# A four-layer convolution, attention and scan kernel: layer 2's products with C moved to GpSimd, its sums over states to adding transfers, softmax reciprocals sent through DRAM

## The chip, the cores and the metric

The kernel runs on one core of a Trainium2 chip. The metric is the device time of one execution in microseconds (us). A core has five engines that matter here: PE (TensorE, matmuls; its weight loads are counted apart as PEld), DVE (VectorE), ACT (ScalarE), POOL (GpSimd) and SP, which here only issues transfers. Each engine works through its own instructions strictly in the order of the program. Sixteen DMA engines move data. "Granted clock" is the mean TensorE clock that the throttle granted, as a share of full speed.

## The reference, cut to what matters

The input has 4 images of 128 channels and 64 x 64 pixels. Four layers follow one another:

```python
x = attention(x)         # layer 0: q, k of 16 channels, softmax over 4096 pixels, v of 128; gamma * out + x
x = two_convs(x)         # layer 1: two 3x3 convolutions with 4-bit weights and activations
x = mamba(x)             # layer 2: selective scan, 256 inner channels, 16 states, then group norm, silu, + x
x = attention(x)         # layer 3: the same with 64 channels, then a product with wo, + x
# softmax: p = exp(e); out = (p @ v) / p.sum()          one sum and one reciprocal per pixel
# layer 2, for every inner channel d and state n, over 4096 steps t:
#   h[t] = dA[t] * h[t-1] + dt[t] * x[t] * B[t, n]
#   y[t] += h[t] * C[t, n]                               summed over the 16 states
```

## The kernel before

The program cuts each image in 8 blocks of 512 pixels. Attention (layers 0 and 3) is 512 tiles of work for PE and ACT. Layer 2 is 32 blocks x 16 states = 512 steps `m`, each on a tile of 128 x 1024 (256 channels x 512 pixels). It runs beside the attention and the convolutions of other images. The last image's layer 3 can only run when its layer 2 is done.

The order of instructions on each engine is made ahead, in Python, by a small list scheduler. Every chain of work yields an engine, a time and what it needs; the chain with the earliest start wins, with 0.15 us of handicap for each unit of its rank. A transfer is an operation of 0.1 us on SP with an assumed landing time `lag`. Only the order goes into the program. At run time the hardware keeps the order, whether the assumed times were right or not.

```python
    @staticmethod
    def op(engine, time, *needs, bank=False, table=None, port=False, lag=0.0): ...
    # in run():
                key = start + load + self.RANK * item[0]         # RANK = 0.15
                if best is None or key < best[0]:
                    best = key, start, load, item
    # ... one (rank, chain) pair for each part of the program
            (3, scans()),
            (3, additions()),
            (3, fetches()),
```

Layer 2's step is three chains: DVE multiplies by B, multiplies the step before by C and makes two scans; GpSimd adds the product to y; ACT copies the last column, where the next block's scan starts.

```python
    def lasts():
        # ... for every step m that is not in an image's last block
                yield op("ACT", 0.2, ("s", m, 1))                # after the second scan
                nc.scalar.copy(hlast[:, n, :], hss[m][:, :, TB - 1])
    def readout(m):
        hs = hss[m]
        nc.vector.tensor_mul(hs, hs, bcs.pop(m)[:, 1:2, :].to_broadcast([P, 2, TB]))     # C
    def scans():
        # ... for every step m
            hss[m] = hs = pair("hs", "hs", 3)
            nc.vector.tensor_mul(hs, ud, bcs[m][:, 0:1, :].to_broadcast([P, 2, TB]))     # B
            if m:
                yield op("DVE", 1.22, ("last", m - 1), port=True)
                readout(m - 1)
            for h in range(2):
                nc.vector.tensor_tensor_scan(hs[:, h, :], das.pop((m, h)), hs[:, h, :], ...)
    def additions():
        # ... for every step m
            nc.gpsimd.tensor_tensor(y, y, hss.pop(m), ALU.add)
```

The sums of the softmax lie in rows 0, 32, 64 and 96 of `ss`. PE gathers them into columns, DVE takes the reciprocal, PE spreads it over all rows:

```python
    def finish(s, c, us, ss):
        # 4 matmuls  sc[:, k] = ss[:, 128k : 128k+128].T @ sel4
        nc.vector.reciprocal(r, sc[:, 0:4])
        # 4 matmuls  sc[:, 128k : 128k+128] = broadcast(r[:, k]).T @ ident
        nc.vector.tensor_mul(us, us, sc)
```

Before each accumulation of p @ v, PE also writes zeros to the accumulator with matmuls of a zero tile.

## Time and profile before

| | before |
|---|---|
| median of 3 runs (lowest, highest) | 3715.16 us (3711.8, 3719.31) |
| profiled run, granted clock | 3718.9 us, 0.967 |
| busy in 240 to 3360 us (3120 us): PE, DVE | 2879.0, 2895.0 us |
| DMA share there | 0.40 |

The prediction shows the busy table, three stretches, the chain and the groups that the change removes. Here are three groups that it leaves, as the page's fifth part lists them: line, engine, operation, output from inputs, shapes, count, busy us, mean ns of one, then the idle time just before and its main releaser.

```profile
L1026 DVE TENSOR_TENSOR_SCAN hs<-da,hlast,hs 128x512 f32<-128x512 f32 x896 | 1102.3, 1264 | 45.5 <-ACT da L991 45.2
L1018 DVE TENSOR_TENSOR hs<-ud,bc 128x1024 f32<-128x1024 f32 x512 | 656.9, 1283 | 0.0
L1001 ACT COPY hlast<-hs 128x2 f32<-128x2 f32 x448 | 85.4, 191 | 130.9 <-DVE hs L1026 129.1
```

The product with B takes 1.28 us and the scan 1.26. DVE spends nearly no time waiting in these groups.

### The profile page before, as it was taken

Reading aid. Unit: us, or ns where it says so; the run is one execution under the profiler, and the core shown is the slowest. Engines: PE = TensorE matmul, PEld = TensorE weight load, DVE = VectorE, ACT = ScalarE, POOL = GpSimd, SP = SyncE. Lnnn points to the kernel's source line nnn. Section 1 sums busy time; section 2 is a strip of 40 time slices with the busy share of each in tenths; the row PEclk is TensorE's granted clock in tenths of the full one; section 3 lists DMA queues with packets and bytes.
Section 4 is the critical chain, followed back from the end, with each engine's and each line's share of the span. In section 5 each row is a group of like instructions: output and inputs, shape, how many; then the busy total and the mean of one; then the engine's idle time right before and its main releaser. Section 6 shows DMA issues by size and latency. Waiting matters only on the chain.

```text
span 3718.9 us, 70774 instructions
## 1 busy us (share of the span) xinstructions
PE 3406.0 (92%) x29874; PEld 2235.8 (60%) x29879; DVE 3104.3 (83%) x2944; ACT 2513.0 (68%) x3656; POOL 1314.1 (35%) x568
## 2 busy tenths in 40 slices
PE   5999979989989999999888999999899989998998
PEld 3776656666666666655545666665555545565665
DVE  3369999999999999899988999999789888893333
ACT  3467767777787777777677767767777777774443
POOL 0014434444434444344433444443344444441000
PEclk8999999999999999999999999999999999999999
DMA  2023334333443334443443333343434444331000
GB/s 70 1 53 96 91 103 100 90 95 92 117 102 97 94 87 95 112 107 101 106 114 102 89 91 92 88 112 87 107 95 108 119 91 108 101 104 63 13 19 17
DMA packets 203658, 327.82 MB, mean 88 GB/s; under 512 B 50609, under 2 KB 53441, under 8 KB 203329
## 3 DMA queue, kind: packets, MB, share of 16 engines
q1 hardware_dynamic: 196384, 322.09, 34.7%
q8 instruction: 236, 3.87, 0.4%
q10 hardware_dynamic: 6944, 1.10, 0.2%
q14 instruction: 94, 0.76, 0.1%
HBM read 304.27 MB, written 18.87 MB: 87 GB/s over the span
## 4 chain that ended last, share of the span: by engine, by line
PE 61%; DVE 21%; ACT 10%; issue 5%; DMA 2%; ACTq 0%; SPq 0%; DVEq 0%
PE us L571 25%; PE e L494 14%; DVE hs L1026 9%; PE us L591 7%; DVE hs L1018 4%; DVE hs L1008 3%; PE conv L686 2%; ACT da L991 2%; ACT p L513 2%; PE xh L775 2%; PE sc L651 2%; PE yo L905 1%; PE sc L638 1%; PE proj L465 1%; PE proj L423 1%
## 5 line engine op out<-in xcount | busy, mean ns | idle before, releaser
L1043 POOL TENSOR_TENSOR y<-y,hs 128x1024 f32<-128x1024 f32 x512 | 1215.3, 2374 | 2050.1 <-DVE hs L1008 2033.6
L571 PE MATMUL us<-p,v 128*32 128x256 f32 (+1 forms) x12288 | 1521.7, 389 | 128.3 <-ACT p L513 128.1
L571 PEld LDWEIGHTS us<-p,v 128*32 128x32 f32 (+1 forms) x12288 | 1009.0, 138 | 550.1 <-ACT p L513 153.5
L513 ACT ACTIVATE p<-e 128x1024 f32<-128x1024 f32 x1024 | 1002.0, 1019 | 383.2 <-PE e L494 255.5
L1026 DVE TENSOR_TENSOR_SCAN hs<-da,hlast,hs 128x512 f32<-128x512 f32 x896 | 1102.3, 1264 | 45.5 <-ACT da L991 45.2
L991 ACT ACTIVATE da<-dt,amat 128x512 f32<-128x512 f32 x1024 | 701.1, 690 | 266.8 <-DVE hs L1026 263.0
L1008 DVE TENSOR_TENSOR hs<-hs,bc 128x1024 f32<-128x1024 f32 x512 | 666.9, 1303 | 34.7 <-ACT hlast L1001 33.8
L1018 DVE TENSOR_TENSOR hs<-ud,bc 128x1024 f32<-128x1024 f32 x512 | 656.9, 1283 | 0.0
L494 PE MATMUL e<-it,v 64*128 64x256 f32 x4096 | 534.6, 402 | 9.2 <-ACT p L513 8.2
L494 PEld LDWEIGHTS e<-it,v 64*128 64x128 f32 x4096 | 386.9, 193 | 155.6 <-issue 89.6
L591 PE MATMUL us<-p,ones 128*32 128x256 f32 x7040 | 469.9, 385 | 0.0
L591 PEld LDWEIGHTS us<-p,ones 128*32 128x32 f32 x7040 | 202.4, 110 | 183.6 <-issue 64.5
L535 DVE TENSOR_TENSOR acc<-p 128x1024 f32<-128x1024 f32 x24 | 29.4, 1225 | 225.4 <-PE us L591 192.6
L494 PEld LDWEIGHTS e<-it,j 64*128 64x128 f32 x2048 | 141.5, 190 | 101.9 <-issue 69.1
L494 PE MATMUL e<-it,j 64*128 64x256 f32 x2048 | 196.5, 310 | 5.1 <-ACT p L513 3.4
L1001 ACT COPY hlast<-hs 128x2 f32<-128x2 f32 x448 | 85.4, 191 | 130.9 <-DVE hs L1026 129.1
L535 DVE TENSOR_TENSOR acc<-p,acc 128x1024 f32<-128x1024 f32 x96 | 117.4, 1223 | 61.6 <-ACT p L513 58.1
L1026 DVE TENSOR_TENSOR_SCAN hs<-da,hs 128x512 f32<-128x512 f32 x128 | 149.9, 1204 | 8.6 <-ACT da L991 8.5
L775 PEld LDWEIGHTS <-w 128*128 128x128 bf16 x576 | 51.4, 98 | 98.3 <-issue 54.3
L775 PE MATMUL xh<-x,w 128*128 128x512 fp8e4 x384 | 95.3, 385 | 1.1 <-ACT sz L798 0.4
L1047 POOL TENSOR_TENSOR y<-y,sz 128x1024 f32<-128x1024 f32 x32 | 95.2, 2976 | 2.5
L465 PE MATMUL proj<-L_conv_wvT,x_in 128*128 128x128 f32 (+1 forms) x512 | 67.7, 288 | 22.9 <-DVE it L410 13.2
(162 smaller groups left out, 2617.3 us busy)
## 6 DMA issues: line engine op xcount, KB each, us to landing
bc<-bc_d SPq DMA_DIRECT2D x512, 512.0 KB, 4.9
x_in<-in_x SPq DMA_DIRECT2D x16, 512.0 KB, 4.8
xpad<-in_x SPq DMA_DIRECT2D x32, 256.0 KB, 3.4
x_d<-yo SPq DMA_DIRECT2D x32, 256.0 KB, 2.3
x_in<-x_d SPq DMA_DIRECT2D x16, 512.0 KB, 6.0
o<-x_d SPq DMA_DIRECT2D x32, 256.0 KB, 5.4
out<-o SPq DMA_DIRECT2D x32, 256.0 KB, 2.2
bc_d<-xd SPq DMA_DIRECT2D x64, 32.0 KB, 1.7
```

The lines of the kernel that those rows point to most:

```text
L465: nc.tensor.matmul(to[:, k * d : (k + 1) * d], lhsT=x[:, k // 4, k % 4 * P : (k % 4 + 1) * P], rhs=wv, start=True, stop=True,)
L494: nc.tensor.matmul(e[k % 4 // 2][:, k % 2, k // 4, :], lhsT=jts[s][row : row + D3, col : col + P], rhs=its[s][row : row + D3, c * CB : (c ...
L513: nc.scalar.activation(p, es[t][h], AF.Exp)
L535: nc.vector.tensor_add(accs[k], ps[t, h], other)
L571: nc.tensor.matmul(us[rows, 0, :], lhsT=vts[s][:, 8 * q + k, cols], rhs=ps[t, h][:, k % 2, k // 4, :], start=False, stop=False,)
L591: nc.tensor.matmul(us[32 * m : 32 * m + 32, 1, :], lhsT=ones[:, 0:32], rhs=term, start=False, stop=q == NQ - 1 and k >= len(terms) - 4,)
L775: nc.tensor.matmul(g, lhsT=w3[:, k // len(rhs), lhs[k % len(rhs)] : lhs[k % len(rhs)] + P], rhs=x[:, rhs[k % len(rhs)]], start=(k == 0), s ...
L991: nc.scalar.activation(da, live["in", g][0][:, h, :], AF.Exp, scale=amat[:, h, n : n + 1])
L1008: nc.vector.tensor_mul(hs, hs, bcs.pop(m)[:, 1:2, :].to_broadcast([P, 2, TB]))
L1018: nc.vector.tensor_mul(hs, ud, bcs[m][:, 0:1, :].to_broadcast([P, 2, TB]))
L1026: nc.vector.tensor_tensor_scan(hs[:, h, :], das.pop((m, h)), hs[:, h, :], hlast[:, n, h : h + 1] if g % NTB else 0.0, ALU.mult, ALU.add,)
L1043: nc.gpsimd.tensor_tensor(y, y, hss.pop(m), ALU.add)
```

## The change

Its intent is to take work off DVE (the product with C) and off PE (reciprocals and zero products), to let GpSimd do the product and the DMA engines the sum over states. Ranks and some buffers change with it.

```diff
+    def readouts():
+        for m in range(NM):
+            g, n = divmod(m, DS)
+            yield op("POOL", 2.36, ("s", m, 1), ("last", m), port=True)
+            hs = hss[m]
+            nc.gpsimd.tensor_tensor(
+                hs, hs, bcs.pop(m)[:, 1:2, :].to_broadcast([P, 2, TB]), ALU.mult
+            )
 ...
+            yield op("POOL", 0.9, *need, lag=7.5)
 ...
+            nc.gpsimd.dma_start(
+                out=sums[g][n % 3],
+                in_=hss.pop(m),
+                accum_op=ALU.bypass if n in (1, 2) else ALU.add,
+            )
 ...
+    def gates():                      # DVE adds the three tiles, GpSimd multiplies by silu(z)
 ...
```

The product writes over `hs`, so it has to wait (`("last", m)`) until ACT has copied the last column.

```diff
@@ finish (softmax reciprocals)
-        # the 8 matmuls shown above
+        yield op("SP", 0.1, ("evict", 2 * k + 1), lag=2.2)
+        nc.sync.dma_start(out=s_d, in_=us[0:P:32, 1, :])                       # 4 rows to DRAM
+        yield op("SP", 0.1, ("s_d", k), lag=2.5)
+        nc.sync.dma_start(out=st, in_=s_d.rearrange("g (p e) -> p g e", e=4))  # back, 128 rows
+        yield op("DVE", 0.3, ("st", k))
+        nc.vector.tensor_reduce(r, st.rearrange("p g e -> p e g"), AX.X, ALU.add)
+        nc.vector.reciprocal(r, r)
+        yield op("SP", 0.1, lag=2.2)
+        nc.sync.dma_start(out=r_d.rearrange("(p e) -> p e", e=4), in_=r)       # to DRAM
+        yield op("SP", 0.1, ("r_d", k), *([("end", k - 1)] if k else []), lag=3.5)
+        nc.sync.dma_start(out=rb, in_=r_d.unsqueeze(0).to_broadcast([P, TB]))  # back, to all rows
+        yield op("DVE", 0.75, ("rb", k), port=True)
+        nc.vector.scalar_tensor_tensor(us, us, scale, rb, ALU.mult, ALU.mult)
@@ products
-                        nc.tensor.matmul(flat(us)[...], ..., rhs=zero.to_broadcast([P, TB]), start=True, ...)
-                            start=False,
+                            start=q == 0 and k < (1 if layer == 0 else 2),
@@ ranks: for example
-            (3, scans()),
-            (3, additions()),
-            (3, fetches()),
+            (1, scans()),
+            (6, readouts()),
+            (0, gates()),
+            (-1, fetches()),
```

Layer 2's output also goes to DRAM and back ahead of the group norm (32 stores and 32 loads of 256 KB), which frees the room for four buffers of `hs` and `bc` instead of three.

## The prediction

> **What bounds the kernel now.** I read the busy table first, then the same table cut into three stretches, because the program has three parts with different limits.
>
> ```profile
> PE 3406.0 (92%) x29874; PEld 2235.8 (60%) x29879; DVE 3104.3 (83%) x2944; ACT 2513.0 (68%) x3656; POOL 1314.1 (35%) x568
> ```
> ```profile
> 0.00:240.00 240.00, 190.60 (x1143) 143.38 (x1145) 86.35 (x140) 100.67 (x117) 3.60 (x24) 0.96 0.15 36
> 240.00:3390.00 3150.00, 2902.19 (x24957) 1895.75 (x24959) 2907.11 (x2696) 2268.32 (x3371) 1310.51 (x544) 0.97 0.40 99
> 3390.00:3719.00 329.00, 313.25 (x3777) 196.66 (x3777) 110.81 (x110) 143.99 (x169) 0.00 (x0) 0.98 0.08 24
> ```
>
> The columns of the second fence are stretch, length, busy us of PE, PEld, DVE, ACT, POOL, then granted clock, DMA share, GB/s. Until 240 us only the attention of layer 0 runs. From 240 to 3390 us layer 2's scans run on DVE beside attention and convolutions on PE, and both engines are busy 92% of 3150 us (2902 and 2907). After 3390 us only the last layer-3 attention is left and PE is 95% busy (313 of 329). PE is thus within 5 to 8% of full everywhere, and DVE is nearly as full in the middle. The chain of waits agrees: PE carries most of it, DVE a fifth.
>
> ```profile
> PE 61%; DVE 21%; ACT 10%; issue 5%; DMA 2%; ACTq 0%; SPq 0%; DVEq 0%
> ```
>
> Next the groups that the change touches (line, engine, operation, operands, count, busy us, mean ns, idle before and its releaser):
>
> ```profile
> L1043 POOL TENSOR_TENSOR y<-y,hs 128x1024 f32<-128x1024 f32 x512 | 1215.3, 2374 | 2050.1 <-DVE hs L1008 2033.6 <-DVE gmean L930 3.1 <-DVE gv L942 3.0
> L1008 DVE TENSOR_TENSOR hs<-hs,bc 128x1024 f32<-128x1024 f32 x512 | 666.9, 1303 | 34.7 <-ACT hlast L1001 33.8
> L651 PE MATMUL sc<-ident,rall 128*128 128x128 f32 x512 | 74.5, 290 | 10.1 <-DVE rall L647 10.1
> L638 PE MATMUL sc<-sel,ss 128*128 128x1 f32 x512 | 72.7, 253 | 11.2 <-ACT ss L619 9.6 <-ACT dt L872 1.6
> L553 PE MATMUL us<-zero,w 128*32 128x512 bf16 x256 | 25.6, 389 | 4.6 <-ACT ss L619 4.6
> L553 PE MATMUL us<-zero,w 128*128 128x512 bf16 x59 | 22.8, 386 | 21.4 <-ACT ss L619 21.4
> ```
>
> GpSimd waits 2034 us for DVE's products with C: it has room. The softmax reciprocals and the zero products are PE work, not idle time.
>
> A fourth view, the timeline around 1305 us, shows how GpSimd and DVE share: the tensor_scalar of L741, 427 ns at its median, began during GpSimd's addition and ended only after it.
>
> ```profile
> 1305.34 2.68 POOL L1043 TENSOR_TENSOR y<-y,hs 128x1024 f32<-128x1024 f32 x1 [9.92 <-DVE hs L1008]
> 1305.83 2.47 DVE L741 TENSOR_SCALAR q<-q 128x512 f32<-128x512 f32 x1
> ...
> 1341.02 2.45 DVE L1026 TENSOR_TENSOR_SCAN hs<-da,hlast,hs 128x512 f32<-128x512 f32 x2
> 1341.24 2.38 POOL L1043 TENSOR_TENSOR y<-y,hs 128x1024 f32<-128x1024 f32 x1 [3.29 <-DVE hs L1008]
> ```
>
> Two scans (one operand in PSUM) took 2.45 us under an addition of 2.38 us, so scans pass beside GpSimd[...].
>
> **What the Trainium skill says.** "SBUF — State Buffer", section "SBUF: two separate sides", calls the pair of ports that DVE and GpSimd share an exclusive lock held for a whole instruction, against DVE work in a 2-port mode or with two SBUF inputs; the 2.47 us of L741 agree. "GPSIMD Engine Reference", section 3.1, puts a two-input fp32 operation at about 2.6 cycles an element at 1.2 GHz, that is 1024 x 2.6 / 1.2 = 2.2 us; the trace has 2.37, and a product should cost what the addition did. "DMA: Bandwidth & Descriptors", section "SWDGE vs HWDGE vs iDMA", says that accumulation during a transfer exists only for transfers issued by GpSimd, whose cores write the descriptors in software; no transfer of the kernel before shows that. "Collectives: The Full Stack", section "The bandwidth ceiling: the fold count and why AG ≠ RS ≠ AR", says that an adding transfer reads two sources and so moves at half the rate of a copy; unseen here as well.
>
> **The change part by part.** (a) Layer 2's products with C leave DVE: -667 us there. They take GpSimd 512 x 2.37 = 1213 us in place of the additions' 1215. The additions become 512 transfers of 512 KB issued by GpSimd; each issue perhaps 1 us (my guess; no such issue is in this trace), so GpSimd goes to 1314 + 512 = 1.83 ms, well below the span. DVE gets two additions per block for merging the three tiles, 64 x 1.22 = 78 us. DVE is left with 3104 - 667 + 78 = 2515 us. The lock is relieved less, as the 2.37 us stay: before, a state's step holds it for 1.28 + 1.30 + 2.37 = 4.95 us, after for 1.28 + 2.37 = 3.65 us. That is about the 1.28 + 2 x 1.26 = 3.80 us that DVE needs for one product and two scans, and the GpSimd product fits under two scans as the addition did.
>
> (b) PE loses the reciprocals' matmuls and the zero products: 74.5 + 72.7 + 25.6 + 22.8 = 196 us, to 3406 - 196 = 3210 us. This is the part on the path. In the view by line PE stood idle just ahead of these three groups (matrix multiply and weight load each) for about 140 us more. The wait for the accumulator's eviction passes to the first real product, while the waits between the two reciprocal steps vanish; I count 55 us of the 140 as gained. One eviction instead of two per block of 256 columns also shortens that wait (128 x about 0.25 us = 32 us of ACT).
>
> (c) The reciprocals now go by four small transfers in series. From the transfers seen (2.2 to 3.5 us to landing) this is some 10 us per chunk. There are 8 chunks a stage and a chunk takes PE some 37 to 43 us, so it is hidden, except for the last chunk: +10 to 12 us at the end, where today the reciprocal and its broadcast take 3.5 us. The residual is now loaded after it, into the same tile, which belongs to the same 12.
>
> (d) Layer 2's output yo now goes to DRAM and back, 32 stores and 32 loads of 256 KB; in groups of four buffers this adds perhaps 10 us ahead of each layer-3 stage. Listing the instruction order of both programs, the last group norm stands before attention tile 448 of 512 in the kernel before and 445 in the changed one, and tile 448 is the first that needs it. So the new order has a little slack there, about 3 tiles of some 5 us.
>
> (e) New ranks move the mix, not the amount of work.
>
> Sum from PE: 3719 - 196 - 55 + 12 = 3480 us. A middle stretch in which DVE is less full should cut some of PE's remaining 8% idle there (248 us); but waits of the in-order ACT queue and lock collisions remain, so I credit 10 us only. As a check, a PE total of 3210 us at today's mean share of 92% gives 3490, and at the last stretch's 95% gives 3380. I say 3470.
>
> **The rivals.** First, the transfers become the bound. Today they take 0.40 of the middle stretch, or 1260 us of the sixteen engines, mostly 512 broadcasts of 512 KB: 34.7% of 3719 us moved 322 MB, so a 512 KB copy takes about 2.1 us. At the half rate of the skill an adding transfer costs 4.2, and 448 of them with 64 plain copies come to 1882 + 134 = 2016 us. With 1260 and some 130 us for small ones that is 3400 us, more than the middle stretch. Against it: the broadcasts are 2 KB rows from DRAM, while the additions move 4 KB rows inside SBUF, and the engines reach only 250 GB/s busy in this trace, so more transfers in flight should fill them better. If it holds, layer 2 paces the program at 6.4 us a state: 512 x 6.4 + 250 + 330 = 3860 us, slower. I give it about one in eight, half of it partial.
>
> Second, the lock or GpSimd paces layer 2: product 2.4, issue 1 to 2, collisions with DVE work. At 5.5 us a state layer 2 would end at 250 + 2816 = 3070 us and the program near 3410, so PE still decides; only beyond 6 us a state (3650) would the gain go.
>
> Third, PE was the bound all along and DVE's relief is worth nothing: then only part (b) counts and the result is 3480 to 3530. A fourth, that DVE was the true pace and PE followed, would allow 3380 or less.
>
> **Range and chances.** Centre 3470 (about 6.6% less). The lower end, 3370, is PE at 95%; the upper, 3620, is half of the transfer rival. Faster by over 2% means below 3641 us.
>
> **What would show it.** DVE busy near 2500 and PE near 3210, with PE's share at 92 to 94%; GpSimd products near 2.4 us; adding transfers landing in under 10 us and a DMA share of 0.6 to 0.85 in the middle; layer 2's last scan ending by about 3080 us; attention running to within 30 us of the end. It is wrong if the DMA share is near 1 with scans waiting for bc or for hs buffers, if GpSimd is over 90% busy, or if PE's idle time grows by over 150 us.

## More of the kernel before

The next view gives all executions of the scan's line: count, shortest/median/longest ns, first and last start.

```profile
L1026 DVE TENSOR_TENSOR_SCAN hs<-da,hlast,hs x896: 1244/1269/1284, 339.6 to 3360.1; 128x512 f32<-128x512 f32 x180
```

The last scan starts at 3360.1 us and the program ends 359 us later. In that tail PE is busy for 336.4 us: it is the attention of the last image. So the end is "last scan plus a tail".

Below, "layer 2's end" is the start of the last scan, and "tail" is the profiled span minus it.

## The result, and the profile after

Ratios in this document are the mean time of one kernel's runs over that of the other's of the same rounds, so they are not quite the ratio of the medians quoted.

The changed kernel took 3816.85 us (median of 4, 3809.09 to 3828.25) against 3715.11 in the same rounds: ratio 1.0276, 95% interval 1.0246 to 1.0306. It is slower by 2.8%, where a gain of 6.6% was predicted. The comparison with the reference passed (e8 below shows that it does not see every error of layer 2).

The busy table of the page:

```profile
PE 3328.3 (87%) x28535; PEld 2139.7 (56%) x28535; DVE 2894.9 (76%) x2560; ACT 2487.6 (65%) x3533; POOL 1883.0 (49%) x1074
```

PE lost only 78 us, not 196, and its idle time grew from 313 us (3719 - 3406) to 483 (3811 - 3328). DVE is 380 us above the predicted 2515. POOL comes out near the prediction (1883 against 1.83 ms), but partly by luck: its products took 1395 us where 1213 were predicted, and the issues 433 where 512 were. The same stretches as before, the middle one now up to the last scan (columns as in the prediction's second fence):

```profile
240.00:3442.00 3202.00, 2797.95 (x23221) 1789.95 (x23221) 2680.57 (x2267) 2216.06 (x3237) 1874.20 (x1053) 0.94 0.79 189
3442.00:3811.00 369.00, 339.59 (x4165) 207.53 (x4157) 128.88 (x153) 173.14 (x187) 5.58 (x3) 0.97 0.17 44
```

Up to the last scan the program is 82 us longer (3202 against 3120), the tail 10 us (369 against 359). So the loss is in layer 2's stretch. DVE's account there: before, 2895 busy and 225 idle; after, 2681 busy and 521 idle. With the product with C gone (-667) and the merging additions new (+78) it should have been 2306 us busy. It has 375 us of extra busy time and 296 of extra idle time. These two have to be explained.

The chain of waits, which the prediction leant on, shows this for the changed kernel:

```profile
PE 7%; DMA 0%; DVE 0%; ACT 0%; issue 0%; DVEq 0%
```

The shares add up to 7%: followed back from the end, the chain breaks off within the last stage, so this view says nothing about the middle. The reading goes on with groups.

The groups of the changed kernel that answer to the scan, the product with B and the addition, with the new issues of transfers:

```profile
L1032 POOL TENSOR_TENSOR hs<-hs,bc 128x1024 f32<-128x1024 f32 x512 | 1394.6, 2724 | 1230.3 <-ACT hlast L996 1122.5
L1014 DVE TENSOR_TENSOR_SCAN hs<-da,hlast,hs 128x512 f32<-128x512 f32 x896 | 1110.2, 1271 | 150.4 <-ACT da L986 113.1
L1008 DVE TENSOR_TENSOR hs<-ud,bc 128x1024 f32<-128x1024 f32 x512 | 783.8, 1531 | 39.3 <-issue 15.7
L1042 POOL DMA_DIRECT2D odd<-hs x320 | 263.4, 823 | 175.2 <-POOL hs L1032 89.6
```

The scans have not changed (1271 ns against 1264). The product with B takes 1531 ns instead of 1283, and GpSimd's product 2724 ns where its addition took 2374. Both engines lose time in the same operations: they collide. And the releaser of GpSimd's work is no longer a DVE product but ACT's copy of the last column (1122.5 us of waits).

The timeline of the changed kernel around 1350 us (start, duration, engine, operation, idle time and releaser) shows both kinds of collision:

```profile
1349.41 1.22 DVE L1008 TENSOR_TENSOR hs<-ud,bc 128x1024 f32<-128x1024 f32 x1
1349.75 3.10 POOL L1032 TENSOR_TENSOR hs<-hs,bc 128x1024 f32<-128x1024 f32 x1
...
1354.46 2.65 POOL L1032 TENSOR_TENSOR hs<-hs,bc 128x1024 f32<-128x1024 f32 x1
1355.85 2.36 DVE L1008 TENSOR_TENSOR hs<-ud,bc 128x1024 f32<-128x1024 f32 x1 [2.31 <-issue]
```

The first GpSimd product began while DVE was in its product with B and was stretched to 3.10 us; at 1355.85 it was DVE that came second, and its 1.2 us became 2.36. In the kernel before, the prediction's own timeline had shown the addition of 2.38 us lying almost wholly under two scans.

The same happened to other DVE operations. In the view by line of all DVE groups, L869 is the subtraction that was L883 before (39.1 us, 1220 ns), and L722 is the addition that was L738 (23.3 us, 729 ns):

```profile
L869 DVE TENSOR_TENSOR ud<-ud,y 128x1024 f32<-128x1024 f32 x32 | 67.7, 2116 | 1.0
...
L722 DVE TENSOR_TENSOR q<-q,xpad 128x512 f32<-128x512 f32 x32 | 45.8, 1432 | 24.5 <-ACT q L719 24.5
```

The idle time is found in the view of waits (engine and line, what was waited for, total us, times, longest):

```profile
ACT da L986 <- DVE hs L1014: 454.3, 261, 7.9
...
DVE us L638 <- DMA rb<-r_d: 143.5, 41, 8.9
...
DVE rall L626 <- DMA st<-s_d: 90.5, 21, 17.5
```

DVE waits 234 us (143.5 + 90.5) for two of the four small transfers of the reciprocals, of which the kernel before has none; there the same steps waited 98 us for PE (84.6 and 13.0). Counted up to the last scan, these steps waited 192 us after and 79 before, and the scans waited 127 us for ACT's decays, against 54. That is 186 of the 296 us of extra idle time; the rest is spread over smaller waits. One such wait in the timeline:

```profile
2022.35 1.28 DVE L1014 TENSOR_TENSOR_SCAN hs<-da,hlast,hs 128x512 f32<-128x512 f32 x1
2031.24 0.18 DVE L626 TENSOR_REDUCE rall<-st 128x4 f32<-128x16 f32 x1 [7.61 <-DMA st<-s_d]
```

A reduction of 0.18 us stood at the head of DVE's queue 7.6 us before its data came, and the next scan, which was ready, stood behind it. ACT's decays, which wait for scans, paid as well (454.3 us against 263.0 before).

Last, the DMA queues of the changed kernel (packets, MB, share of sixteen engines' span; q0 carries what GpSimd issues):

```profile
q1 hardware_dynamic: 258336, 356.84, 34.7%
q0 software_dynamic: 73728, 268.47, 33.7%
```

The DMA share of the middle doubled from 0.40 to 0.79, but is not full.

### The profile page after: what moved, and what is told of

It reads as the page before. It is cut to its first block, busy times and chain, and to the rows that moved or that the text cites.

```text
span 3810.9 us, 69427 instructions
## 1 busy us (share of the span) xinstructions
PE 3328.3 (87%) x28535; PEld 2139.7 (56%) x28535; DVE 2894.9 (76%) x2560; ACT 2487.6 (65%) x3533; POOL 1883.0 (49%) x1074
## 5 line engine op out<-in xcount | busy, mean ns | idle before, releaser
L1032 POOL TENSOR_TENSOR hs<-hs,bc 128x1024 f32<-128x1024 f32 x512 | 1394.6, 2724 | 1230.3 <-ACT hlast L996 1122.5
L556 PE MATMUL us<-p,v 128*32 128x256 f32 (+1 forms) x12288 | 1544.1, 394 | 141.3 <-ACT us L599 76.4
L556 PEld LDWEIGHTS us<-p,v 128*32 128x32 f32 (+1 forms) x12288 | 1027.6, 140 | 597.4 <-issue 163.2
L1014 DVE TENSOR_TENSOR_SCAN hs<-da,hlast,hs 128x512 f32<-128x512 f32 x896 | 1110.2, 1271 | 150.4 <-ACT da L986 113.1
L986 ACT ACTIVATE da<-dt,amat 128x512 f32<-128x512 f32 x1024 | 694.8, 691 | 470.0 <-DVE hs L1014 454.3
L1008 DVE TENSOR_TENSOR hs<-ud,bc 128x1024 f32<-128x1024 f32 x512 | 783.8, 1531 | 39.3 <-issue 15.7
L1042 POOL DMA_DIRECT2D odd<-hs x320 | 263.4, 823 | 175.2 <-POOL hs L1032 89.6
L996 ACT COPY hlast<-hs 128x2 f32<-128x2 f32 x448 | 85.3, 190 | 216.1 <-DVE hs L1014 215.0
L1042 POOL DMA_DIRECT2D y<-hs x192 | 169.3, 882 | 62.9 <-POOL hs L1032 60.4
L1058 POOL TENSOR_TENSOR y<-y,sz 128x1024 f32<-128x1024 f32 x32 | 99.4, 3105 | 106.2 <-DVE y L1055 87.8
```

The lines of the kernel that those rows point to most:

```text
L556: nc.tensor.matmul(us[rows, 0, :], lhsT=vts[s][:, 8 * q + k, cols], rhs=ps[t, h][:, k % 2, k // 4, :], start=q == 0 and k < (1 if layer == ...
L986: nc.scalar.activation(da, live["in", g][0][:, h, :], AF.Exp, scale=amat[:, h, n : n + 1])
L1032: nc.gpsimd.tensor_tensor(hs, hs, bcs.pop(m)[:, 1:2, :].to_broadcast([P, 2, TB]), ALU.mult)
L1042: nc.gpsimd.dma_start(out=sums[g][n % 3], in_=hss.pop(m), accum_op=ALU.bypass if n in (1, 2) else ALU.add,)
L1058: nc.gpsimd.tensor_tensor(y, y, live.pop(("sz", g)), ALU.mult)
```

## The experiments

The theory after this reading (**T**): two things made the loss. (1) GpSimd's product is released by ACT's copy at a moment that has nothing to do with DVE's cycle, so it meets DVE's products instead of lying under the scans. (2) The scheduler was told 2.2 to 3.5 us for the four small transfers; they take longer, and DVE waits at the head of its queue. Rivals: **R1**, the adding transfers slow everything (my first rival in the prediction); **R2**, the removal of work from PE and DVE is worth little, because the order and not the amount of work sets the pace; **R3**, the new ranks did the damage.

Sixteen kernels ran. All times are medians of runs, 4 of each unless noted; before was 3714 to 3715 us in every batch. The changed kernel was timed in one batch only, so the experiments are compared with it across batches. Layer 2's end and the tail are from each kernel's profile.

| run | us | ratio [95%] | layer 2's end | tail | PE share, clock |
|---|---|---|---|---|---|
| before | 3715 | 1 | 3360 | 359 | 92%, 0.967 |
| after | 3816.9 | 1.0276 [1.0246, 1.0306] | 3442 | 369 | 87%, 0.946 |
| e1_recip_pe | 3774.9 | 1.0169 [1.0151, 1.0187] | 3305 | 464 | 90%, 0.962 |
| e2_att_only | 3783.0 | 1.0185 [1.0168, 1.0202] | 3440 | 343 | 87%, 0.944 |
| e3_c_dve | 4084.0 | 1.1002 [1.0984, 1.1021] | 3725 | 352 | 80%, 0.906 |
| e4_c_into_bc | 3975.9 | 1.0692 [1.0654, 1.0730] | 3626 | 353 | 83%, 0.918 |
| e5_nozero | 3738.9 | 1.0064 [1.0047, 1.0081] | 3383 | 356 | 91%, 0.966 |
| e6_lags | 3743.1 | 1.0066 [1.0046, 1.0087] | 3381 | 369 | 88%, 0.952 |
| e7_half_add | 3696.2 | 0.9946 [0.9930, 0.9963] | 3330 | 372 | 89%, 0.959 |
| e8_half_product | 3639.2 | 0.9792 [0.9772, 0.9812] | 3275 | 366 | 90%, 0.957 |
| e9_nozero_same_order (14 runs) | 3705.5 | 0.9977 [0.9969, 0.9985] | 3347 | 355 | 91%, 0.968 |
| e10_before_half_c | 3664.8 | 0.9862 [0.9846, 0.9879] | 3302 | 362 | 93%, 0.971 |
| e11_last_dve | 3689.7 | 0.9933 [0.9917, 0.9950] | 3279 | 405 | 89%, 0.957 |
| e12_last_dve_lags | 3569.8 | 0.9601 [0.9581, 0.9622] | 3195 | 388 | 91%, 0.969 |
| e13_last_dve_recip_pe | 3599.5 | 0.9679 [0.9655, 0.9703] | 3096 | 504 | 93%, 0.974 |
| e14_old_ranks | 4082.6 | 1.0989 [1.0971, 1.1007] | 3593 | 487 | 83%, 0.923 |
| e15_att_lags (12 runs) | 3712.6 | 0.9995 [0.9986, 1.0003] | 3372 | 341 | 88%, 0.953 |
| e16_best_half_add | 3470.2 | 0.9335 [0.9319, 0.9351] | 3087 | 388 | 93%, 0.978 |

One warning for reading it. Any edit of a chain makes the scheduler form a new order, and a new order by itself moves the time. e9 and e5 give a rough measure: both remove the same zero products, e9 with the times told to the scheduler left as they were, e5 with new times. They differ by 33 us, 0.9%; but e5 also has one eviction copy instead of two, so not all of this need be the order, and nothing shows that an order can't do more. So differences below 1% between kernels of different order are not read as the effect of a part, and those of 1 to 2% only where the waits that were aimed at changed too and the same edit gave a gain in other kernels. e7, e8, e9, e10 and e16 keep the order of the kernel that they start from.

### Which moment GpSimd's product is released at: e11, e4, e3, e8

**e11_last_dve.** The last column is copied by DVE instead of ACT, right behind the next step's product with B. GpSimd's product, which needs that copy, is then released just as DVE turns to two scans.

```diff
-    def lasts():                       # ACT, after the second scan
+    def last(m):
+            yield op("DVE", 0.12)
+            nc.vector.tensor_copy(hlast[:, n, :], hss[m][:, :, TB - 1])
     def scans():
             nc.vector.tensor_mul(hs, ud, bcs[m][:, 0:1, :]...)      # B, step m
+            if m:
+                yield from last(m - 1)
             for h in range(2):         # two scans
```

> The changed kernel, with the copy of the last column (which GpSimd's product must wait for) taken from ACT to DVE and placed right behind the next state's product with B, so that GpSimd's product is released when DVE turns to two scans, as the addition was in the kernel before. If the moment of release is what makes the lock collide: GpSimd's product is back to 2.4-2.5 us (2.72 now), DVE's product with B to 1.2-1.35 us (1.53), and the time falls by 80-180 us to 3640-3740. If only the amount of GpSimd work under the lock matters: 3790-3850 us, since DVE also gets 448 copies of about 0.15 us.

Measured: 3689.7 us, 127 less than the changed kernel. Its groups:

```profile
L1033 POOL TENSOR_TENSOR hs<-hs,bc 128x1024 f32<-128x1024 f32 x512 | 1253.6, 2448 | 1254.2 <-DVE hlast L995 1152.0
...
L1007 DVE TENSOR_TENSOR hs<-ud,bc 128x1024 f32<-128x1024 f32 x512 | 657.3, 1284 | 49.2 <-DMA bc<-bc_d 24.1
```

The product with B is back at 1284 ns, GpSimd's product at 2448, though DVE got 126 us of copies more (448 x 281 ns). DVE's busy time up to layer 2's end fell from 2681 to 2509 us, and layer 2 ended 163 us earlier. So part (1) of T is shown as far as the collisions go: their length follows the moment of release. How much of the 127 us is due to them is less sure. The edit also frees ACT of the 448 copies: 85.3 us of work, ahead of which ACT waited 215.0 us for scans. (Its decays then waited 521.6 us for scans, 454.3 in the changed kernel.) A run that relieves ACT alone was not made.

**e4_c_into_bc.** The other way round: GpSimd writes its product over the `bc` tile instead of `hs`, so that it needn't wait for the copy of the last column and the second scan itself releases it.

```diff
-            yield op("POOL", 2.36, ("s", m, 1), ("last", m), port=True)
-            nc.gpsimd.tensor_tensor(hs, hs, bc[:, 1:2, :]..., ALU.mult)
+            yield op("POOL", 2.36, ("s", m, 1), port=True)
+            nc.gpsimd.tensor_tensor(bc, hs, bc[:, 1:2, :]..., ALU.mult)
```

> The changed kernel, with GpSimd's product written over the tile of B and C instead of over hs, so that it need not wait for ACT's copy of the last column (GpSimd waited 1122 us for that copy). If the late, irregular release by ACT is what makes GpSimd collide with DVE: products start right behind the second scan, lie under DVE's next scans or product in a fixed pattern, and the time falls by 60-150 us to 3670-3760. If GpSimd runs into DVE's product with B whatever releases it: no gain, 3780-3850 us.

Measured: 3975.9 us, outside both ranges. A wait was taken away and the time grew by 159 us. GpSimd's product took 2841 ns and the product with B 1539: released at the end of the scans, it meets the product with B that follows them, as here:

```profile
1299.31 1.20 DVE L1010 TENSOR_TENSOR hs<-ud,bc 128x1024 f32<-128x1024 f32 x1
1299.49 3.22 POOL L1034 TENSOR_TENSOR bc<-hs,bc 128x1024 f32<-128x1024 f32 x1 [6.21 <-DVE hs L1016]
```

Also the `bc` tile is now held until its transfer has read it, and DVE waited 128.3 us for bc (15.7 in the changed kernel). So e4 is not a clean test of the phase alone, but it shows that an earlier release is no gain in itself.

**e3_c_dve.** The product with C is put back on DVE; GpSimd only issues the transfers.

```diff
-            nc.gpsimd.tensor_tensor(hs, hs, bcs.pop(m)[:, 1:2, :]..., ALU.mult)
 # in scans(), as in the kernel before:
+            if m:
+                yield op("DVE", 1.22, ("last", m - 1), port=True)
+                readout(m - 1)
```

> The changed kernel, with the products with C put back on DVE; GpSimd only issues the adding transfers. Lock theory (collisions of GpSimd's product with DVE work make DVE's instructions longer, 1.53 us for a product of 1.28): the product with B is back at 1.2-1.25 us, and GpSimd's one remaining product per block leaves few collisions; DVE has 667 us more to do but loses 250-380 us of lengthening, so 3780-4000 us. Transfer theory: DMA does the same as in the changed kernel and the time stays within 40 us of 3817.

Measured: 4084.0 us, above both ranges. The collisions are gone (product with B 1205 ns, with C 1219; in the kernel before, with its additions on GpSimd, they took 1283 and 1303), and DVE has 3065 us of work, less than in the kernel before. Still the program takes 369 us more than that kernel. DVE waited 190.3 us for rb, 74.4 for st and 109 for ACT's steps of the convolutions. Taking the product off DVE is therefore a real gain within the changed design; why this kernel is so far behind the kernel before, which has the same products on DVE, is answered in part only by its waits, and stays open for the rest.

**e8_half_product.** The changed kernel in the same order, GpSimd's product on half the columns (wrong; the comparison with the reference still passed, as it did for e7, e10 and e16, so it doesn't see this error).

```diff
-                hs, hs, bcs.pop(m)[:, 1:2, :].to_broadcast([P, 2, TB]), ALU.mult
+                hs[:, 0], hs[:, 0], bcs.pop(m)[:, 1, :], ALU.mult
```

> The changed kernel, in the same order, with GpSimd's product with C done on half of the columns only (about 1.25 us instead of 2.72 us); the result is wrong on purpose. Lock theory: DVE's product with B falls from 1.53 to under 1.35 us, DVE loses 150-250 us of lengthening, and the time falls to 3650-3750 us. Transfer theory: 3790-3825 us. If PE's own work and its waits for ACT set the time by now: no more than 40 us gained.

Measured: 3639.2 us, 178 less. GpSimd's product took 1588 ns, the product with B 1319, DVE's busy time fell from 2895 to 2659 us. GpSimd was busy 49% of the time in the changed kernel and no bound, and DVE's waits for st and rb did not shrink (103.1 and 154.8 us). So this gain is read as one of the lock: the shorter it is held, the less DVE loses.

### The small transfers of the reciprocals: e6, e12, e1, e13, e2, e15

**e6_lags.** Only the assumed landing times are raised; no instruction changes, only the order.

```diff
-        yield op("SP", 0.1, ("evict", 2 * k + 1), lag=2.2)
+        yield op("SP", 0.1, ("evict", 2 * k + 1), lag=4.5)
 # the other three in the same way: 2.5 -> 5.0, 2.2 -> 4.0, 3.5 -> 6.5
```

> The changed kernel, with only the landing times that its scheduler assumes for the four transfers of the reciprocals raised from 2.2, 2.5, 2.2 and 3.5 us to 4.5, 5.0, 4.0 and 6.5 us, near what the trace shows under load; this moves the waiting DVE instructions later in DVE's queue. If the loss from the reciprocals (42 us, from e1_recip_pe) is DVE waiting for transfers at the head of its queue: DVE's waits for st and rb fall from 234 to under 100 us and the time to 3740-3790 us. If the loss is something else: 3800-3840 us.

Measured: 3743.1 us, 74 less than the changed kernel. DVE's waits for st and rb fell from 234 to 129 us (51.4 + 77.2), not under 100 as expected. Four numbers that are not even in the program were worth 74 us, through the order that is made from them. One new order could be lucky; that the same edit also gave 70 us on e2 (e15) and 120 on e11 (e12) speaks for part (2) of T.

How long the transfers take can be read from SP's issues: the load from DRAM waits for the store before it. The median from issue to issue was 4.2 us in the changed kernel (1.7 at best, 6.3 at the ninetieth percentile, 12.9 at worst). In e2, where the adding transfers are absent and the DMA share is 0.40, it was 1.8 (4.1 at the ninetieth). Some of these gaps hold other issues; where none stands between (42 and 46 of the 64), the medians are 4.55 and 2.14. For the second pair it was 3.4 against 3.0 us. So the 2.2 us told to the scheduler were about right without the adding transfers.

**e12_last_dve_lags.** e11 and e6 together.

```diff
+ e11's edit and e6's edit
```

> e11_last_dve together with the landing times of e6_lags. If the two losses add up (release of GpSimd, DVE waiting for the reciprocals' transfers): 74 us less than e11_last_dve, 3560-3670 us, which would beat the kernel before. If DVE's pace no longer matters by then: no more than 30 us less than e11_last_dve.

Measured: 3569.8 us, 4.0% faster than the kernel before and 6.5% faster than the changed one. This is the fastest version that computes the whole sum. The line of its scans, and two lines of its timeline (DVE, then GpSimd):

```profile
L1015 DVE TENSOR_TENSOR_SCAN hs<-da,hlast,hs x896: 1247/1273/1285, 384.3 to 3195.0; 128x512 f32<-128x512 f32 x180
```
```profile
1343.82 2.46 DVE L1015 TENSOR_TENSOR_SCAN hs<-da,hlast,hs 128x512 f32<-128x512 f32 x2
...
1343.89 2.35 POOL L1033 TENSOR_TENSOR hs<-hs,bc 128x1024 f32<-128x1024 f32 x1 [0.87 <-DVE hlast L995]
```

GpSimd's 2.35 us lie under two scans of 2.46: what the prediction took for granted is here made true. Layer 2 ends at 3195 us instead of 3442. Separately the two edits gave 127 and 74 us, together 247: with the collisions gone, a DVE that waits less can perhaps use the time better (a reading, not tested).

**e1_recip_pe.** The changed kernel with the reciprocals back on PE.

```diff
-        # four small transfers, tensor_reduce
+        # the 8 matmuls of the kernel before
+        nc.vector.scalar_tensor_tensor(us, us, scale, sc, ALU.mult, ALU.mult)
```

> The changed kernel, with only the softmax reciprocals put back on PE (two groups of four small matmuls a chunk). Theory A, DVE's queue stands still behind the reciprocals' transfers (it waited 143.5 us for rb and 90.5 us for st in the changed kernel): these waits go, at most some 30 us for PE's results takes their place, and the time falls from 3817 to 3640-3720 us although PE gets about 150 us of work back. Theory B, the adding transfers or the lower granted clock set the pace: no gain, 3790-3870 us.

Measured: 3774.9 us, 42 less than the changed kernel, though PE gets its 147 us of matmuls back. This lies between the two ranges. The waits for transfers went, but 157.5 us of waits for PE (121.6 and 35.9) took their place, where I had allowed 30; 49 us of them fall before layer 2's end. Layer 2 ends 137 us earlier (3305), but the tail is 464 us instead of 369: the attention of layer 3 has fallen behind.

**e13_last_dve_recip_pe.** e11 with the same edit as e1.

```diff
+ e11's edit and e1's edit
```

> e11 (last column copied by the vector engine, so that GpSimd's product begins under the scans) with the softmax reciprocals back on the tensor engine as before. If the head-of-queue waits on the small transfers are what e11 still loses (228 us of waits for st and rb), they vanish here and the time is near that of the run with corrected landing times, 3570 us, plus at most some 60 us for the 147 us of matmuls that PE gets back: 3570 to 3640. If the corrected times helped for another reason (a luckier order), this kernel stays near e11's 3690.

Measured: 3599.5 us, as the first theory there says. It makes the two sides of the reciprocals visible. Against e12, layer 2 ends 99 us earlier: up to there DVE waited 37 us for PE in these steps, where e12 waited 110 for the transfers (and its busy time is 49 us less):

```profile
L1023 DVE TENSOR_TENSOR_SCAN hs<-da,hlast,hs x896: 1247/1276/1286, 348.8 to 3096.1; 128x512 f32<-128x512 f32 x180
```

But the tail is 504 us, with PE busy for 486 of them (96%):

```profile
3096.00:3600.00 504.00, 485.94 (x5987) 307.14 (x5979) 130.40 (x152) 226.39 (x244) 7.59 (x5) 0.99 0.10 31
```

Here PE is the bound, and the 116 us longer tail takes back more than layer 2 gained. So the reciprocals through DRAM are worth 30 us (0.8%) once layer 2 runs well, but the two kernels have different orders, so this is at the edge of what can be told.

**e2_att_only** and **e15_att_lags.** The kernel before with the changed attention alone: reciprocals through DRAM, no zero products, one eviction; layer 2 and ranks as before. e15 has e6's landing times as well.

```diff
  # kernel before
- parts(), residual(), finish() and the zero products of before
+ those of the changed kernel
+ (e15 only) lag=4.5, 5.0, 4.0, 6.5
```

> The kernel before, with only the attention part of the change: reciprocals through DRAM, no zero products, one eviction copy instead of two; layer 2, its ranks and its tiles as before. If PE bounds the kernel before (my prediction), PE loses 196 us of work and the time falls to 3500-3600 us. Theory A (DVE paces layer 2, layer 2 paces the end): DVE waits 100-200 us for the reciprocals' transfers and the time is 3715-3880 us, no faster although PE has less to do. DMA share stays near 0.4 and the clock near 0.967.

> e2 (the kernel before with the changed attention part only, 3783 us) with the assumed landing times raised as in e6. If the loss of e2 is the vector engine waiting at the head of its queue for small transfers (88 + 72 us), most of it goes: 3690 to 3720 us, with waits for st and rb under 60 us each. If the loss of e2 was a poorer order as such, it stays above 3750 us.

Measured: 3783.0 and 3712.6 us. On its own this part cost 68 us with the landing times as assumed (DVE waited 87.8 us for st and 71.6 for rb), and with better times it is worth nothing at all: 0.9995, although PE's busy time fell from 3406 to 3275 us and DVE's waits for st and rb to 35.2 and 12.7. On this layer 2, PE's saved work bought nothing. It is not a test of PE's work alone, since DVE's busy time rose by 50 us at the same time (3104.3 to 3154.0).

### The traffic of the adding transfers: e7, e16

**e7_half_add** and **e16_best_half_add.** The changed kernel, and e12, in unchanged order, with the accumulating transfers moving half the columns. Their outputs are wrong, which doesn't matter for the times.

```diff
+            cut = slice(0, 2 if n in (1, 2) else 1)
             nc.gpsimd.dma_start(
-                out=sums[g][n % 3],
-                in_=hss.pop(m),
+                out=sums[g][n % 3][:, cut],
+                in_=hss.pop(m)[:, cut],
```

> The changed kernel, in the same order, with each accumulating transfer moving only half of its columns (256 KB instead of 512 KB); the result is wrong on purpose. Transfer theory: DMA share of the middle falls from 0.78 to about 0.62, the small transfers land sooner, and the time falls by 60-120 us to 3700-3760. Lock theory: it stays at 3785-3825 us.

> The best version (3570 us) with the accumulating transfers moving half the columns, wrong on purpose, same order. In the changed kernel this gave 120 us. If the traffic costs only through the latency of the small transfers at the head of the queue, and the corrected times hide that, the gain here is small: under 35 us (3535 to 3575). If traffic costs by itself (scans or GpSimd waiting for landings, slower accesses), the gain is again 60 us or more: under 3510 us.

Measured: 3696.2 us for e7 (120 less than the changed kernel) and 3470.2 for e16 (100 less than e12). I had expected e16 to gain under 35 us if the traffic costs only through waits that the better landing times hide; that was wrong. But the waits were not hidden in e12: DVE still waited 84.2 us for st, 81.6 for rb and 35.2 for bc. In e16 these are 55.3, 60.4 and 5.5, together 80 us less, and layer 2 ended 108 us earlier. Up to layer 2's end DVE's idle time fell by 96 us, 74 of them in these three waits. GpSimd's product (2445 and 2447 ns) and the scans (1270 and 1271) did not get faster. So R1 is right in part: the traffic costs 100 to 120 us, in e12 mostly through the landing times of other transfers that DVE waits for, while the DMA engines aren't full (share 0.83 in e12, 0.71 in e16).

### What sets the end: e9, e5, e10

**e9_nozero_same_order** and **e5_nozero.** The kernel before without the zero products; in e9 the times told to the scheduler are unchanged, so that ACT, DVE and SP keep their order. e5 has new times and also one eviction copy instead of two.

```diff
-                        nc.tensor.matmul(flat(us)[...], ..., rhs=zero..., start=True, stop=False)
-                            start=False,
+                            start=q == 0 and k < (1 if layer == 0 else 2),
 # e5 only, besides the single eviction copy
-                time = (1.93 if layer == 0 else 0.95) + (0.3 if need else 0.0)
+                time = 1.93 if layer == 0 else 0.95
```

> The kernel before, without the zero products, and with the scheduler's times left as they were, so that the order on every engine stays that of the kernel before. If PE's work is on the path: 3715 less 48 us of matmuls and up to 66 us of idle time in front of them, 3610-3670 us. If PE only follows a pace set elsewhere: 3695-3720 us; then the 0.6% lost in e5_nozero came from the new order, not from the products.

> The kernel before, with only two of the small parts: no zero products (the first real product starts the accumulation) and one eviction copy instead of two; reciprocals stay on PE, layer 2 as before. If PE's work is on the path: PE loses 48 us of work and up to 66 us of idle time in front of it, 3610-3670 us. If DVE's layer 2 is the pace and PE only follows: 3690-3730 us.

Measured: e9 3705.5 us, 9 less. The prediction counted 48 us of matmuls for these products and put them on the path; PE's busy time fell by 26.5 us (3406.0 to 3379.5), and 9 came through. e5 was 24 us slower than before, outside both ranges: work was removed, and a new order seems to have cost more than that.

**e10_before_half_c.** The kernel before in the same order, DVE's product with C on half the columns. Its output is wrong, which doesn't matter for the time.

```diff
-        nc.vector.tensor_mul(hs, hs, bcs.pop(m)[:, 1:2, :].to_broadcast([P, 2, TB]))
+        nc.vector.tensor_mul(hs[:, 0], hs[:, 0], bcs.pop(m)[:, 1, :])
```

> The kernel before, in the same order, with DVE's products with C on half of the columns only (about 0.65 us instead of 1.30 us, 330 us less DVE work); the result is wrong on purpose. If DVE paces the middle of the kernel before: 3715 less 150 to 330 us, 3380-3560 us. If PE is the bound with DVE beside it, as the prediction had it: 3660-3715 us.

Measured: 3664.8 us. DVE lost 270 us of work (3104.3 to 2834.0) and the program 50. Layer 2 ended 59 us earlier (3301.5), the tail was the same (362). DVE waited more elsewhere (151.4 us for the sums of the softmax, 84.6 before). The time lies in the range that I had given for the prediction's theory, PE as the bound with DVE beside it (3660 to 3715), and not in that for DVE as the pace. Yet e9 shows as little for PE: 26.5 us less work there, 9 gained. I read both as R2: in fixed orders that tie four engines together, less work on one of them is given away as waits to a large part. No run shows a single engine as the pace of the kernel before.

### The new ranks: e14

**e14_old_ranks.** The changed kernel with the ranks of the kernel before on all chains that both have; readouts and gates, which are new, get 3 as the additions had.

```diff
-            (2, parts()), (1, scans()), (6, readouts()), (0, gates()), (-1, fetches()), ...
+            (1, parts()), (3, scans()), (3, readouts()), (3, gates()), (3, fetches()), ...
```

> The changed kernel with the ranks of the kernel before on every chain that both have (new chains get the rank of the additions). If ranks move only the mix, as I predicted, the time stays within 1% of the changed kernel (3780 to 3855 us). If the new ranks were chosen to make the other parts work, it is slower by more than 2% (over 3890 us). If the new ranks are part of the loss, it is faster by more than 2% (under 3740 us).

Measured: 4082.6 us, 266 more than the changed kernel. R3 falls: the new ranks are not the loss, they save 266 us (6.5% of 4083). Its waits:

```profile
POOL odd L1042 <- DVE y L1055: 330.5, 43, 17.6
DVE rall L626 <- DMA st<-s_d: 307.6, 44, 30.6
```

GpSimd's issues wait 330 us for DVE's merging additions (81 in the changed kernel), which now come late (rank 3 instead of 0), and DVE waits 308 us for st (90.5). Which of the ranks matters most was not tried.

## Why the prediction was wrong, step by step

**The bound: "PE is thus within 5 to 8% of full everywhere", and part (b): "This is the part on the path".** This step failed first. "Everywhere" was a misreading: until 240 us PE is busy 190.6 of 240 us, 79%, by the prediction's own fence. And a busy share of 92% is no proof of a path. Layer 2's end plus a tail of 340 to 405 us gives the end of the program in all kernels but three; the exceptions are e1, e13 and e14, whose tails are 464 to 504 us with PE busy 94 to 96% of them, as attention lags there. The prediction put 196 us of matmuls and 55 us of waits on the path. With landing times that fit, the attention part bought nothing on the old layer 2 (e15, 0.9995), and 48 us of zero products bought 9 (e9). Where layer 2 is fast enough, PE does count: e13's tail. The kernel before sat close to both limits, and I read only one. My third rival, PE as the bound all along (3480 to 3530), fails on e9 and e15 in the same way; the fourth, DVE as the true pace, fails on e10, where 270 us less work on DVE gave 50.

**Part (a): "the GpSimd product fits under two scans as the addition did".** This was the costliest error. I compared durations (3.65 us against 3.80) and not moments. The addition fitted since DVE's own product released it as DVE turned to its scans; the new product is released by ACT's copy. DVE's busy time up to layer 2's end became 375 us more than the prediction's sum gives. e11, which restores the moment, got 127 us back and the product to 2448 ns. (The prediction's 2.2 us for a GpSimd operation was an estimate; e12's timeline shows a product of 2.35 us.) The issue times (823 and 882 ns, guessed 1 us) were near, and GpSimd's total was met partly by luck, as said above.

**Part (b), the size.** PE was to fall to 3210 us and was 3328. In e12 it was 3250, at nearly the clock of before (0.969). But the lower clock of the changed kernel (0.946) does not account for its 3328: e3, with the lowest clock of all (0.906), has the same number of matmuls and 3271 us. What lengthened PE's busy time stays open.

**Part (c): "so it is hidden, except for the last chunk".** The landing times were picked too low: 2.2 to 3.5 us were "seen", but the page of the kernel before also lists 5.4 and 6.0 us (median) for loads of what had just been stored to DRAM (o and x_in from x_d). And the 10 us may be hidden from PE, but I didn't ask where the waiting instructions stand. They stand in DVE's queue, in front of scans. The part of the cost that better landing times take back was 74 us (e6), or 120 beside e11's edit (e12 against e11); e12 still waits 166 us for st and rb. The last chunk, with layer 2's round trip of part (d), I put at 12 us and some; the tail grew by 10. The round trip was not tried by itself.

**Part (e): "New ranks move the mix, not the amount of work".** The words are true and the step is wrong: it was given no weight. e14 shows 266 us between two mixes.

**The rivals.** The transfers (first) I gave one chance in eight, as a bound of 3860 us with 4.2 us for each adding transfer. (The sum has a slip: 3400 us over 512 states are 6.6 us and not 6.4, which gives 3980.) The queue's share gives 3810.9 x 0.337 / 512 = 2.5 us each, the DMA share in the middle 0.79, and the products with B waited only 15.7 us for bc. As a bound this rival is wrong; as contention that lengthens other landings it cost 100 to 120 us (e7, e16). The second, layer 2 paced by the lock, named the right thing and dismissed it, since I held PE to be the bound: "only beyond 6 us a state (3650) would the gain go". The kernel before was itself beyond that line: from first to last scan the changed kernel took (3442 - 251) / 511 = 6.24 us a state, the kernel before (3360 - 244) / 511 = 6.10, e12 5.73.

**The sum.** I predicted 3470 and got 3817. Of the 347 us, e12 wins back 247 (the moment of release and the landing times). With half the adding traffic e16 lands at 3470, with PE at 3219 us and layer 2's end at 3087, near the 3210 and 3080 that I had described; but its sums are wrong, and DVE's 2730 us and the tail of 388 are not what I described. So it does not confirm the number, and meeting it is luck.

Of my signs of being wrong one came: PE's idle time grew by 170 us, over the 150 that I had named. The others didn't (DMA share near 1, GpSimd over 90%). The adding transfers landed as expected (7.8 and 7.9 us, median, under 10; DMA share 0.79).

## What to carry to other kernels

Before moving an operation to an engine that shares a lock, ask what will release it and where the other engine stands at that moment; equal durations are not enough. An operation that waits for a transfer costs what stands behind it in its engine's queue, so tell the scheduler landing times that were measured under the load of the new kernel, and look for head-of-queue waits first. A share of busy time near full on one engine doesn't make it the path: look at what the program's end is made of (here layer 2's end and a tail) before pricing saved work.

## What the Trainium skill lacked or had wrong

- "SBUF — State Buffer", section "SBUF: two separate sides", was right on the exclusive lock: a product with B that came second took 2.36 us instead of 1.2, and a GpSimd product that came second 3.10 instead of 2.4. What it lacks is that the releaser of the GpSimd operation decides how often this happens: the mean of the same GpSimd product was 2724, 2841 or 2448 ns with three releasers (after, e4, e11).
- The same section says that a DMA can't be slowed by compute nor the reverse. The runs agree in one direction: half the adding traffic left scans at 1270 and 1271 ns and GpSimd's product at 2445 and 2447 ns (e12, e16). Whether compute slows a transfer was not tested.
- "Collectives: The Full Stack", section "The bandwidth ceiling: the fold count and why AG ≠ RS ≠ AR", gives a ring's ReduceScatter, whose adds read two sources, half the rate of AllGather's copies. The prediction took this over for adding transfers inside SBUF, where a factor of two on the broadcasts' time didn't come out: 2.5 us of sixteen engines for 512 KB, where the broadcasts of the kernel before, from DRAM, took 2.1. The page calls its model specific to rings, so it was my use of it that was wrong. A plain copy of the same form was not measured by itself.
- "DMA: Bandwidth & Descriptors", section "Latency and other measured facts", says that lighter HBM load makes the fixed cost of a transfer smaller. The runs show a growth that this does not cover: a store of 8 KB to DRAM let the next load be issued after 1.8 us (median) in e2 and after 4.2 in the changed kernel, with nearly the same HBM traffic (90 and 94 GB/s). What differed was the traffic inside SBUF: the DMA share is 0.40 and 0.79.
- "TensorE: Matmul & The Clock Gate", section "Part 1: The HAM clock gate (the "warmup" mystery)", ties the clock to how busy PE has been. The table above goes with it: 0.906 at 80%, 0.946 at 87%, 0.967 at 92%, 0.978 at 93%, and e13 has 0.974 with as many adding transfers as the changed kernel. None of the pages that I read gives this relation over a whole kernel. That the clock follows from PE's waits is argued from this, not shown by a run.
